# Six weight matrices turned by VectorE from 32x32 blocks instead of by TensorE, in a transformer block on one Trainium2 core

## The chip, the cores and the metric

The kernel runs on one core of one Trainium2 chip. The metric is device time in microseconds (us) for one execution. The core has five engines that each work through their own instruction list in order: TensorE (PE; its weight loads are listed as PEld), VectorE (DVE), ScalarE (ACT), GpSimd (POOL) and SyncE (SP). They wait for each other by semaphores. DMAs are issued here from SP's list, some at the start from ACT's.

## What is computed

The input x is 16 sequences of 256 tokens with 256 features, all in float32. Each sequence goes through attention with 16 heads, a conditioned RMS norm, an RWKV-like mixing with a scan along the tokens, a rotation, and a gated feed-forward net of 704 hidden units whose inputs and weights are first rounded to blockwise FP4 (16 neighbours share a scale):

```
q, k, v = x @ Wq.T, x @ Wk.T, x @ Wv.T              # 256x256 each
a  = softmax(mask(q k^T / 4)) v @ Wo.T              # 16 heads of 16
xn = rmsnorm(a) * scale * (1 + sc) + shift          # shift, sc from silu(cond) @ Wc.T + bc
x1 = x + wkv(xn; Wk, Wv, Wr, decay, first) @ Wo2.T  # the second set of 256x256 weights
h  = silu(fp4(xr) @ fp4(w_gate).T) * (fp4(xr) @ fp4(w_up).T)   # xr = x1 filtered and rotated; 704x256 weights
out = x1 + fp4(h) @ fp4(w_down).T                   # 256x704
```

Every weight is used transposed, with its input feature on the partitions, so each has to be turned once on the way in.

## The kernel before

The 16 sequences ("batches" b) are pipelined through stages, all written as generators that yield after a few instructions: `ask` (a: load the next x, project q, k, v), `attend` (t), `leave` (l: output projection and norm), `mix` (m), `rotate` (r), `hidden` (h and i, two row halves), `turn_h` (d and e) and `down` (f). Set-up stages bring in the constants: `loads` (L: issue the DMAs of weights and small vectors), `turn_w` (Q for q, k, v; O for o; A for the second set), `turn_mask` (K), `modulate` (M), `rotation` (R), `times` (T), `in_weights` (W0 to W5: gate and up, quantised and turned) and `out_weights` (V0, V1: down).

The string ORDER, written out at the top of the file by a planner, names the stage that is to take its next step. A loop under a manual schedule walks through it, so each engine's list is ORDER's projection on that engine. Nothing reorders it at run time. The instruction that waits holds up everything behind it on its engine.

The lines that the change and the prediction touch (numbers of the kernel before):

- **L143, `load_x`.** x of a batch comes in as four DMAs of 32 partitions with rows of 64 floats (256 bytes). In that layout each 32x32 block lies where VectorE's 32x32 transpose (L605) turns the whole of it into feature-major xT in one instruction. The x buffer has two slots.
- **L216, `load_w`.** The weights q, k, v, o come in as one DMA of 256 KB each with rows of 1 KB, in SP's list. **L224 to L227**: 13 small DMAs of vectors and of the conditioning (tile `rows`) in ACT's list.
- **L301 and L305, `turn_w`.** Four TensorE transposes of 128x128 turn a weight into PSUM and one copy brings it to SBUF: on VectorE for q, k, v, o (L305), on ScalarE for the second set ak, av, ar, ao (L307).
- **L524 to L535, `in_weights`.** Gate and up (1408 rows in all) are taken 256 rows at a time, six times: 12 DMAs, `quant` on 512 columns (the last on 256), 22 TensorE transposes (L531), six ScalarE copies into guT (L535).
- **`quant`, L488 to L500.** First half on VectorE: absolute maximum, scale, reciprocal, multiply (L488, L490, L491, L492). Then ScalarE takes the absolute value into bf16 (L494). Second half on VectorE: two roundings (L496, L497). POOL multiplies the scale back (L500).
- **L313, L315**: `rows` turned by TensorE and copied to `cols`, from which most of the set-up starts. **L318, L323, L329**: the mask made float, turned, reduced. **L352 to L358**: silu of the conditioning on VectorE, and the matmuls that need it. **L433, L439**: the rotation matrix.
- **L567, L579, L656, L677**: projections, scores and attention values on TensorE. The first L579 on oT is `leave(0)`.

The weight tiles borrow buffers that later hold other things. `raw` (gate, up, down on their way in) shares its two buffers with the mask in float.

The build hands the DMAs eight completion semaphores in turn. A DMA's issue waits until the DMA eight places before it (in the program's order over both lists) has landed, so at most eight are in flight.

At the start TensorE runs 12 transposes of the identity matrix into a bank that nobody reads (L184).

Of the kernel before, what the change touches and what calls it, by code (L numbers as in the profile page):

```python
# [27 lines left out]
L L L L W1 L Q Q L K L a0 W5 a0 W1 W1 K K Q Q Q W1 Q a0 L W1 a0 R a0 K a0 L W5 R L W0 W1 K K K W5 A R t0 a0 L A  # L28
W1 O t0 L a0 W3 R W5 W5 W0 M a1 A O t0 A W5 a1 R M a2 W5 t0 t0 t0 a1 R a1 t0 W0 W3 t0 R W3 W3 t0 W2 a1 t0 t0 a1
M a1 t1 a1 W0 A W3 V0 t1 t1 R R A M t0 W0 W3 a2 R t1 W0 V0 M t1 W2 t1 t0 W3 t1 t1 W4 a3 V1 W0 t0 A t0 M t0 t1 V0  # L30
t0 a3 t0 A T W2 W2 t1 T t1 V0 t1 a2 a2 a2 t1 l0 a2 t1 a2 t1 V0 l0 l0 t1 V0 a2 W4 W2 t1 l0 V0 a4 l0 l0 t2 l0 m0
t1 V1 W4 a3 t2 t2 a3 a3 m0 m0 m0 m0 m0 t2 t2 a3 W4 V1 t2 m0 m0 m0 l1 l1 l1 m0 m0 m0 l1 t2 W4 m0 m0 m0 m0 m0 t2
t2 t2 t2 l1 V0 l1 l1 a3 a3 V0 t2 t2 r0 V1 t2 W4 m1 m1 t2 W2 m1 m1 r0 a4 m1 t3 m1 W4 t3 t2 m1 m1 V1 t2 t3 t3 t2
W2 V1 r0 t3 t3 m1 m1 m1 m1 r0 V1 a4 l2 l2 m1 m1 m1 m1 t3 m1 a4 r0 t3 l2 t3 t3 a4 t3 t3 l2 r1 r1 r0 t3 r0 a4 l2
t3 t3 r1 r1 r1 l2 l2 a4 a4 a5 t3 r0 r0 a5 r0 m2 m2 t4 t4 t3 t3 m2 m2 a6 i0 i0 i0 i0 t4 i0 i0 i0 i0 i0 i0 i0 i0
i0 i0 m2 m2 m2 m2 m2 r1 r1 r1 r1 m2 t4 t4 m2 t4 r1 m2 a5 a5 a5 a5 a5 a5 m2 l3 t5 l3 t4 l3 l3 h0 m2 m2 m2 t4 t5
m2 h0 h0 h0 h0 h0 h0 l3 h0 h0 h0 r2 t5 l3 l3 V1 h0 i1 h0 r2 t4 r2 a6 V1 h0 m3 t4 i1 a7 h0 r2 i1 h1 i1 r2 t4 h1
h1 i1 t4 h1 t4 t4 h1 h1 h1 t4 m3 m3 a6 h1 h1 t5 a6 h1 r2 h1 r2 t4 t5 t4 i1 a6 r2 r2 t5 h1 h1 i1 r2 m3 a6 t5 i1
i1 i1 i1 t5 t5 h1 m3 t5 t4 t5 t5 a6 a6 m3 m3 t6 t6 m3 m3 m3 i1 i1 m3 m3 i2 i2 i2 i2 i2 m3 e0 e0 i2 i2 t6 t6 e0
i2 l4 i2 t6 i1 i2 i2 t6 h2 h2 e0 t5 m3 m3 m3 l4 h2 t6 l4 h2 m3 h2 t6 l4 h2 i2 h2 h2 h2 h2 t5 r3 h2 t5 l4 r3 a7  # L40
d0 l4 t5 h2 t6 t5 t5 l4 i2 m4 d0 d0 m4 a8 h2 t6 d0 h2 i2 a7 r3 t6 a7 a7 t6 t6 t6 t6 a7 m4 m4 m4 r3 r3 a7 a7 m4
m4 m4 t7 l5 t7 t7 l5 m4 m4 m4 m4 m4 t6 t7 l5 l5 l5 r3 m4 m4 e1 m4 m4 l5 l5 t7 t6 t6 f0 f0 f0 f0 r4 t7 r3 r4 a8
r3 e1 e1 e1 r3 f0 t7 t7 t7 d1 d1 r4 t7 t7 d1 r3 r4 i3 a9 d1 r4 i3 m5 m5 i3 i3 i3 i3 i3 a8 r4 m5 m5 i3 i3 i3 t7
a8 a8 a8 i3 i3 i3 m5 m5 t8 m5 m5 m5 l6 l6 a8 a8 l6 r4 h3 h3 l6 t8 t8 m5 h3 h3 h3 f1 m5 m5 t8 t8 i3 l6 t8 h3 f1
m5 m5 h3 h3 t7 r4 r4 r4 f1 l6 m5 m5 l6 h3 h3 h3 m5 t8 t8 t7 t7 t7 t7 t8 r5 t8 f1 t8 i4 i4 m6 t8 t8 r5 a9 d2 h3
h3 i4 d2 i4 aa i4 t8 m6 h3 t8 m6 a9 r5 r5 r5 a9 a9 a9 t8 t9 t7 d2 r5 r5 t8 t9 m6 i4 d2 r5 r5 r5 i4 i4 i4 i4 e2
m6 e2 m6 a9 i4 e2 i4 t8 e2 a9 m6 m6 l7 i4 l7 m6 m6 m6 t9 l7 l7 f2 f2 m6 m6 m6 m6 l7 l7 l7 l8 l8 t9 h4 m7 h4 l8
h4 m6 l8 m6 m7 f2 h4 f2 h4 h4 h4 h4 r6 h4 h4 l8 m7 m7 t9 t9 r6 l8 l8 h4 t9 t9 t9 r6 aa e3 f1 r6 i4 i5 h4 t9 e3
e3 e3 h4 i5 i5 i5 i5 t9 m8 r6 i5 m7 i5 i5 h4 r6 aa m7 i5 aa t9 t9 t9 ab t9 m8 i5 i5 i5 d3 f2 m7 r6 d3 h5 h5 h5
h5 h5 aa aa h5 i5 r6 r6 ta t9 h5 t9 h5 m7 h5 ta ta h5 h5 m7 h5 aa ta r6 h5 m8 aa m7 d3 d3 m7 m7 m7 m7 h5 m7 f3  # L50
m7 m7 f3 f3 f3 m8 m8 ta ta ta m8 ta m8 ta r7 r7 m8 m8 m8 ta ta d4 d4 ta i5 ta ta ta ab f3 i6 i6 i6 i6 i6 i6 i6
i6 i6 i6 i6 h6 h6 h6 h6 h6 h6 h6 h6 h6 h6 i6 ab ab ab ab d4 d4 ta tb h6 m8 h6 t9 m8 e4 e4 i6 h6 ab m8 ta ta e4
m8 ac r7 m8 l9 tb m8 i6 ab e4 f4 f4 l9 r7 h6 r7 f4 l9 l9 l9 m8 e5 tb r8 tb f4 l9 l9 f4 r8 d5 ac m9 m9 m9 r8 e5
r8 r7 r7 tb m9 la d5 r7 la la m9 m9 r8 la ac ac m9 m9 m9 m9 m9 r8 r7 tb m9 d5 m9 r7 ac m9 la d5 la la m9 ac tb
m9 tb tb i7 ma ma tb tb ad i7 i7 i7 i7 i7 i7 i7 i7 e5 e5 i7 i7 i7 tb tc tc tc m9 r8 i7 f5 f5 i7 ma f5 f5 d6 f5
r8 d6 r9 tb h7 r9 tb h7 ad r8 tb ma r8 h7 h7 h7 h7 r9 r9 h7 h7 h7 ma ma tb r9 ma r9 tc tc tc tb h7 h7 h7 ad ad
tb r9 ac ac ma ma ma ma ma h8 h8 h8 tc ma ma d6 h8 h8 d6 tc ad i8 ma ma ad r9 i8 i8 i8 i8 i8 i8 h8 h7 h8 tc i8
i8 i8 h7 ma h8 e6 h8 e6 e6 e6 h8 lb h8 h8 r9 f6 lb i8 i8 r9 f6 h8 f6 f6 ra i8 lb lb lb f6 tc tc ra e7 lb lb e7
tc h8 i8 i9 tc i9 i9 i9 ae tc ra tc mb e7 i9 mb ad ra ra td d7 e7 i9 ad tc ra i9 ae d7 td td mb mb ra tc i9 tc
i9 mb td td h9 ra i9 mb i9 mb td mb h9 mb h9 i9 h9 h9 h9 mb h9 h9 h9 d7 d7 td h9 h9 td td i9 h9 h9 lc lc td lc  # L60
af mb ae ra mb lc f7 mb mb i9 ae lc lc ra mb f7 mb lc mc ia mc h9 ia ia ia ia f7 f7 ia ia ia td ia ia ia ia mb
rb rb td td d8 td ae rb f7 ia td rb ae ae mc d8 te td mc d8 mc ae rb ia d8 rb td e8 mc td mc mc af mc e8 e8 e8
mc mc mc rb mc ld mc mc f8 te mc te te rb rb ld ld ld te ha f8 f8 ha mc ha ha rb te ha f8 ha ha ha te ha ib ha
ha ha te te te te te ib ha rc ib ib ib ib ib ib ld ld ld te rc ha ib rc ib ib e9 hb d9 rc md e9 af te rc md hb
ib hb f8 te hb md hb ib e9 md d9 af te te af e9 hb rc rc ib rc te C md af hb hb hb hb hb d9 d9 tf md af af md rc
rc hb hb le le md md tf f9 tf le md md f9 le md tf md md md md md tf tf ic ic ic ic ic f9 f9 ic ic ic le hb rd
ic le ic tf ic rd le ic me f9 rd tf ic da tf rd rd da ea hc ea hc hc rd ea ic me hc da ea tf hc rd hc tf da me
me me me tf tf hc rd me hc hc tf tf hc hc me me hc me tf tf rd tf hc me fa me me me me fa fa rd db fa me lf id
db lf fa id id id id lf lf id id id me db id id id hc lf C hd hd lf db hd lf id hd hd eb re id eb eb hd hd mf mf
id eb hd re re hd fb re hd dc hd re fb fb mf re dc fb hd mf fb mf mf re hd mf ec ec ec dc dc mf ec re fc hd mf  # L70
fc mf fc mf mf ed re fc dd fc ed mf re dd mf mf mf mf ed ie ed ie ie ie ie ie ie ie dd rf dd ie ie he C he ie he
rf rf ie C rf he ie he ie he rf fd he he he rf rf rf fd he fd he rf ee fd rf if if he he if ee if if he if if if
if hf hf if hf if if hf ee ee fd hf if hf de if hf hf hf de de de hf hf fe hf hf fe hf fe fe ef ef ef fe ef df
df df df ff ff ff ff ff
# [4 lines left out]
def kernel(  # L79
# [58 lines left out]

    def load_x(b):
        if b < B:  # L140
            t = io.tile([P, S // 32, 64], F32, tag="x", name="x_sb", bufs=2)
            for a in range(4):
                queue[0].dma_start(  # L143
                    out=t[32 * a : 32 * a + 32], in_=x[b].rearrange("(q i) (a c) -> a i q c", i=32, a=4)[a]
                )
            x_sb[b] = t
# [36 lines left out]
    for i in range(12):  # L183
        nc.tensor.transpose(warm[:, 0:P], ident, ident)  # L184
# [24 lines left out]
    def loads():  # L209
        def load_w(name, src, tag, bufs=1):  # L210
            w_in[name] = lent(tag, bufs)
            if name == "ao":

                nc.sync.dma_start(out=w_in[name], in_=src.rearrange("(p h) c -> p h c", h=2))
            else:
                nc.sync.dma_start(out=w_in[name], in_=src.rearrange("(t p) c -> p t c", p=P))  # L216
# [3 lines left out]
        load_w("q", w_q, "ek")  # L220
        yield
# [10 lines left out]
        yield  # L232
        load_w("v", w_v, "kv")
# [58 lines left out]
    def turn_w(*names):  # L292
        for name in names:
            t = w_in.pop(name)
            pt = ps()
            for ct in range(E2):
                for ot in range(E2):
                    part = t[:, ot, ct * P : (ct + 1) * P]
                    if name in ("q", "k", "v"):
                        part = half(t[:, ot, :], ct)  # L300
                    nc.tensor.transpose(pt[:, ct * E + ot * P : ct * E + (ot + 1) * P], part, ident)  # L301
            yield
            wT[name] = wts.tile([P, E2, E], F32, tag="wt_" + name, name="wt_" + name)
            if name in ("q", "k", "v", "o"):
                nc.vector.tensor_copy(flat(wT[name]), pt)  # L305
            else:
                nc.scalar.copy(flat(wT[name]), pt)  # L307
            yield
# [205 lines left out]
    def in_weights(j):  # L514
        j *= 2 * P
        nt = min(2, (2 * FF - j) // P)
        n = nt * E
        raw = wk.tile([P, FF], F32, tag="h", name="raw", bufs=2)[:, 0:n]
        for jj in range(nt):
            lo, hi = j + jj * P, j + (jj + 1) * P  # L520
# [434 lines left out]
    for j in range(6):  # L955
        stages[f"W{j}"] = lambda j=j: in_weights(j)
# [159 lines left out]
```

## Time and profile before

| what | value |
|---|---|
| time, median of 3 runs | 677.73 us (676.33 to 678.62) |
| the profiled execution: its own time | 678.29 us |
| the profiled execution: its span | 676.4 us (1.9 us of the time lie around it) |
| granted TensorE clock, mean | 0.998 |
| DMA moved | 13.63 MB in 37,327 packets, 32,900 of them under 512 bytes |
| busiest TensorE lines | L880 (gate and up) 163.9 us, L656 (scores) 74.0, L934 (down) 70.7, L677 (values) 61.7 |
| transposes that the change concerns, on TensorE | L301 on q, k, v, o: 16; L531 on gate and up: 22 |
| last TensorE instruction ends | at 671.1 us |

How to read it: a busy time is the sum of an engine's instructions. The chain of waits follows the last instruction back, at each step to what released it, and so shows which engine set the end. A window table gives each engine's busy time in a stretch. TensorE's instructions overlap, so a mean duration of one (0.27 us for a 128x128 transpose late in the set-up) is longer than its share of the chain (0.11 us).

### The profile page before, as it was taken

The page shows a single profiled execution, that of the slowest core. Times are in us where ns is not written, and L with a number is a line of the kernel's source. Part 1 is how long each engine was busy: PE and PEld are TensorE (multiplying, and loading weights), DVE is VectorE, ACT ScalarE, POOL GpSimd, SP SyncE. Part 2 cuts the span into 40 slices and gives each one's busy share as a digit, 9 for nine tenths or more (in the row PEclk, how much of TensorE's full clock was granted, in tenths as well). Part 3 has the DMA queues.
Part 4 walks back from the last instruction along what each step waited for, and adds up shares of the span by engine and source line. Part 5 has one row for each costly group of instructions (what it writes and reads, how often), then busy time and mean ns, then how long its engine had stood idle before and what let it go on. Part 6 is the DMA issues. An engine that isn't in the chain of part 4 may idle for free.

```text
span 676.4 us, 10441 instructions
## 1 busy us (share of the span) xinstructions
PE 662.4 (98%) x3928; PEld 467.7 (69%) x3928; DVE 580.9 (86%) x973; ACT 353.7 (52%) x777; POOL 147.0 (22%) x171
## 2 busy tenths in 40 slices
PE   6999999999999999999999999999999999999995
PEld 5667666756677766866777767676776677768774
DVE  6887988998897868888989898898998898999971
ACT  1788756564574465555344644273454554343232
POOL 4802311311222021130203120130311313031210
PEclk9999999999999999999999999999999999999999
DMA  5520000000001001010010100010000000001001
GB/s 160 131 69 1 9 9 17 1 16 0 1 17 29 5 1 32 1 25 9 5 28 1 32 5 12 1 32 1 16 1 17 1 0 17 1 16 31 10 9 36
DMA packets 37327, 13.63 MB, mean 20 GB/s; under 512 B 32900, under 2 KB 36884, under 8 KB 37268
## 3 DMA queue, kind: packets, MB, share of 16 engines
q1 hardware_dynamic: 37152, 12.85, 7.6%
q8 instruction: 33, 0.54, 0.3%
q14 instruction: 26, 0.21, 0.1%
q10 hardware_dynamic: 116, 0.02, 0.0%
HBM read 8.67 MB, written 4.19 MB: 19 GB/s over the span
## 4 chain that ended last, share of the span: by engine, by line
PE 90%; DVE 6%; DMA 1%; ACT 1%; issue 0%; SPq 0%; POOL 0%; ACTq 0%; POOLq 0%; DVEq 0%
PE ps L567 24%; PE ps L880 21%; PE pss L656 10%; PE ps L934 9%; PE ps L677 9%; PE ps L579 8%; PE ps L543 3%; PE ps L843 2%; PE ps L917 2%; PE ps L591 1%; DVE v L496 1%; DVE v L497 1%; DVE h L897 1%; DVE am L488 1%; PE ps L301 1%; DVE v L492 1%
## 5 line engine op out<-in xcount | busy, mean ns | idle before, releaser
L880 PE MATMUL ps<-guT,xqT 128*128 128x352 f32 x512 | 163.9, 463 | 0.5 <-ACT xqT L865 0.3
L665 ACT ACTIVATE w<-pss 128x512 f32<-128x512 f32 x256 | 133.7, 606 | 41.5 <-PE pss L656 41.3
L880 PEld LDWEIGHTS ps<-guT,xqT 128*128 128x128 f32 x512 | 94.1, 190 | 55.0 <-issue 3.7
L500 POOL TENSOR_TENSOR hq<-v,am 128x704 f32<-128x704 f32 (+2 forms) x40 | 56.0, 1401 | 203.0 <-DVE v L497 147.0
L656 PE MATMUL pss<-qT,kT 32*128 32x512 f32 x512 | 74.0, 640 | 0.0
L934 PE MATMUL ps<-hT,downT 128*128 128x256 f32 x312 | 70.7, 380 | 0.0
L494 ACT ACTIVATE m<-v 128x704 bf16<-128x704 f32 (+2 forms) x56 | 40.7, 729 | 50.1 <-DVE v L492 40.8
L934 PEld LDWEIGHTS ps<-hT,downT 128*128 128x128 f32 x312 | 58.9, 190 | 10.1 <-DVE h L897 0.8
L677 PE MATMUL ps<-w,v_one 128*32 128x256 f32 x1024 | 61.7, 382 | 0.0
L891 ACT ACTIVATE th<-ps 128x352 f32<-128x352 f32 x64 | 30.2, 472 | 56.2 <-PE ps L880 54.3
L814 DVE RECIPROCAL den<-den 128x512 f32<-128x512 f32 x16 | 53.6, 3348 | 0.5
L496 DVE SCALAR_TENSOR_TENSOR v<-m,v 128x704 f32<-128x704 bf16 (+2 forms) x56 | 47.1, 841 | 5.1 <-ACT m L494 5.1
L677 PEld LDWEIGHTS ps<-w,v_one 128*32 128x32 f32 x1024 | 30.1, 109 | 29.4 <-issue 6.3
L497 DVE SCALAR_TENSOR_TENSOR v<-m,v 128x704 f32<-128x704 bf16 (+2 forms) x56 | 47.1, 841 | 1.9
L546 ACT COPY hT<-ps 128x384 f32<-128x384 f32 (+1 forms) x64 | 27.1, 431 | 40.1 <-PE ps L543 40.0
L893 DVE SCALAR_TENSOR_TENSOR th<-th,ps 128x352 f32<-128x352 f32 x64 | 32.4, 506 | 13.3 <-ACT th L891 13.0
L897 DVE SCALAR_TENSOR_TENSOR h<-th,ps 128x352 f32<-128x352 f32 x64 | 33.3, 520 | 8.2 <-PE ps L880 3.9
L500 POOL TENSOR_TENSOR xq<-v,am 128x512 f32<-128x512 f32 x16 | 18.5, 1154 | 87.4 <-DVE v L497 87.4
L543 PEld LDWEIGHTS ps<-ident,hq 128*128 128x128 f32 (+1 forms) x204 | 23.5, 136 | 18.7 <-issue 4.9
L656 PEld LDWEIGHTS pss<-qT,kT 32*128 32x128 f32 x512 | 20.7, 182 | 22.6 <-issue 18.6
L817 POOL TENSOR_TENSOR yT<-num,den 128x512 f32<-128x512 f32 x16 | 20.6, 1288 | 71.1 <-DVE den L814 56.3
L687 DVE STREAM_TRANSPOSE u<-ps 128x512 f32<-128x512 f32 x32 | 22.5, 704 | 14.3 <-PE ps L677 14.3
(175 smaller groups left out, 1191.9 us busy)
## 6 DMA issues: line engine op xcount, KB each, us to landing
x_sb<-in_x_dram SPq DMA_DIRECT2D x64, 64.0 KB, 2.1
out_dram<-o_sb SPq DMA_DIRECT2D x52, 64.0 KB, 1.8
out_dram<-o_sb SPq DMA_DIRECT2D x6, 128.0 KB, 3.9
raw<-in_L_ffn_w_down_dram SPq DMA_DIRECT2D x2, 352.0 KB
raw<-in_L_ffn_w_gate_dram SPq DMA_DIRECT2D x5, 128.0 KB, 3.0
raw<-in_L_ffn_w_up_dram SPq DMA_DIRECT2D x5, 128.0 KB
ek<-in_L_cond_Wq_dram SPq DMA_DIRECT2D x1, 256.0 KB, 3.0
er<-in_L_cond_Wk_dram SPq DMA_DIRECT2D x1, 256.0 KB
```

The source lines that it names most:

```text
L496: nc.vector.scalar_tensor_tensor(v, m, 1.5 * 2.0**22, v, ALU.max, ALU.add)
L497: nc.vector.scalar_tensor_tensor(v, m, 1.5 * 2.0**22, v, ALU.max, ALU.subtract)
L500: nc.gpsimd.tensor_tensor(blk(dst), blk(v), bc(am), ALU.mult)
L543: nc.tensor.transpose(pt[0:n, (k - k0) * P : (k - k0 + 1) * P], src[:, k * P : k * P + n], ident)
L567: nc.tensor.matmul(pool_tile[:, ot * n : (ot + 1) * n], w[:, ct, ot * P : (ot + 1) * P], src[ct], start=(ct == 0), stop=(ct == E2 - 1),)
L579: nc.tensor.matmul(pool_tile[:, tt * E : (tt + 1) * E], srcT[:, ct, tt * P : (tt + 1) * P], w[:, ct, :], start=(ct == 0), stop=(ct == E2 - 1),
L656: nc.tensor.matmul(quad[r], kT[rows_, g, kt * P : (kt + 1) * P], qT[rows_, g].rearrange("p i q -> p (i q)"), start=True, stop=True,)
L665: nc.scalar.activation(w[:, kt, r].rearrange("p i q -> p (i q)"), quad[r], AF.Exp)
L677: nc.tensor.matmul(pu[32 * r : 32 * r + 32, i * S : (i + 1) * S], vo[:, kt, 8 * g + 2 * r + i, :], w[:, kt, r, i, :], start=(kt == 0), sto ...
L814: nc.vector.reciprocal(flat(den), flat(den))
L880: nc.tensor.matmul(p_[:, 0:FH], xqT[:, ct, tt * P : (tt + 1) * P], guT[:, ct, base + f * FH : base + (f + 1) * FH], start=(ct == 0), stop= ...
L934: nc.tensor.matmul(pdn[:, 0:S], downT[:, k, h * P : (h + 1) * P], hT[:, k, :], start=(k == 0), stop=(k == FK - 1))
```

## The change

Weights q, k, v are loaded like x, in four DMAs of 32 partitions with rows of 256 bytes, and turned by one VectorE transpose each. q and v are issued from ACT's list, v right behind q and ahead of the 13 small vectors; k stays on SP. Weight o is loaded in eight DMAs with rows of 128 bytes and also turned by one VectorE transpose. Gate and up are taken in four parts of 352 rows instead of six of 256: four DMAs each with rows of 256 bytes, `quant` on 704 columns, one VectorE transpose straight into guT, no TensorE and no PSUM. The second set (ak, av, ar, ao) and down are as before. The 12 idle transposes become 18. ORDER is another one throughout.

```diff
+    def in_blocks(t, src, engine):
...
+        for a in range(4):
+            engine.dma_start(out=t[32 * a : 32 * a + 32], in_=src.rearrange("(q i) (a c) -> a i q c", i=32, a=4)[a])
...
-    for i in range(12):
+    for i in range(18):
         nc.tensor.transpose(warm[:, 0:P], ident, ident)
...
+            elif name in ("q", "k", "v"):
+                in_blocks(w_in[name].rearrange("p t (q c) -> p (t q) c", c=64), src, nc.sync if name == "k" else nc.scalar)
+            elif name == "o":
+                for a in range(4):
+                    for h in range(2):
+                        nc.sync.dma_start(
+                            out=w_in[name].rearrange("p t (q h j) -> p h (t q) j", h=2, j=32)[32 * a : 32 * a + 32, h],
+                            in_=src.rearrange("(q i) (h a j) -> a h i q j", i=32, h=2, a=4)[a, h],
+                        )
...
+            if name in ("q", "k", "v"):
...
+                nc.vector.transpose(
+                    as_blocks(flat(wT[name])), by_blocks(t.rearrange("p t (q c) -> p (t q) c", c=64))
+                )
...
+            if name == "o":
...
+                nc.vector.transpose(
+                    as_blocks(flat(wT[name])), t.rearrange("p t (q h j) -> p h (t q) j", h=2, j=32)
+                )
...
-            if name in ("q", "k", "v", "o"):
-                nc.vector.tensor_copy(flat(wT[name]), pt)
-            else:
-                nc.scalar.copy(flat(wT[name]), pt)
+            nc.scalar.copy(flat(wT[name]), pt)
...
     def in_weights(j):
...
+        src = (w_gate, w_up)[j // 2][(j % 2) * FH : (j % 2 + 1) * FH]
+        raw = wk.tile([P, FF], F32, tag="h", name="raw", bufs=2)
+        in_blocks(raw.rearrange("p (q c) -> p q c", c=64), src, nc.sync)
+        yield
+        wq = yield from quant(raw, FF, "hq", 4)
+        nc.vector.transpose(
+            guT[:, :, j * FH : (j + 1) * FH].rearrange("p h (q i) -> p h q i", i=32),
+            by_blocks(wq.rearrange("p (q c) -> p q c", c=64)),
+        )
...
-    for j in range(6):
+    for j in range(4):
         stages[f"W{j}"] = lambda j=j: in_weights(j)
```

The new order changes the lists at the start as follows. In SP's list stand x of batch 0, k, one quarter of gate and up (W1), the mask, x of batch 1, the eight DMAs of o, Wc, ak, av, then W0, x of batch 2, W3, ar, ao. In VectorE's list the first half of W1's `quant` stands ahead of the copy of `cols` and of the mask. In TensorE's list the first projections follow the idle transposes directly, and the silu matmuls stand ahead of the transposes of ar, where they stood behind the rotation's matmuls.

## The prediction

> **What bounds the kernel now.** I read the page first, for which engine is full and where.
>
> ```profile
> span 676.4 us, 10441 instructions
> ...
> PE 662.4 (98%) x3928; PEld 467.7 (69%) x3928; DVE 580.9 (86%) x973; ACT 353.7 (52%) x777; POOL 147.0 (22%) x171
> ...
> PE   6999999999999999999999999999999999999995
> ```
>
> TensorE is busy in every slice but the first and the last. Windows of 15 us (stretch, its length, then busy us of PE, PEld, DVE) sharpen this for the set-up:
>
> ```profile
> 15.00:30.00 15.00, 15.00 (x111) 10.25 (x110) 12.14 (x35) 11.84 (x24) 11.98 (x34) 1.00 0.51 133
> 30.00:45.00 15.00, 15.00 (x138) 9.70 (x141) 12.37 (x28) 12.36 (x27) 3.89 (x3) 1.00 0.31 81
> 45.00:60.00 15.00, 15.00 (x105) 10.04 (x98) 13.16 (x24) 11.57 (x26) 4.28 (x5) 1.00 0.09 22
> ```
>
> PE has 15.00 of 15, and so on to 585 us with 0.1 us missing; after that it loses 1.5 us up to 660 and ends with the last batch's serial tail. So from 15 us on, an instruction taken from TensorE is time saved, and each new wait of TensorE is time lost. VectorE is the next engine, at 12 to 13 of 15. TensorE's waits at the start are the other reserve:
>
> ```profile
> PE ps L301 <- DMA ek<-in_L_cond_Wq_dram: 1.7, 1, 1.7
> PE ps L301 <- DMA kv<-in_L_cond_Wv_dram: 1.5, 1, 1.5
> ```
>
> Last the chain of waits (start, length, what), which is TensorE's list after 11 us. I use three of its marks:
>
> ```profile
> 12.14 4.93 PE ps L567 x16
> ...
> 34.08 0.59 PE ps L301 x4
> ...
> 50.52 3.65 PE ps L579 x16
> ```
>
> 12.14 is the first projection. 34.08 is the point by which TensorE has done the work that the new order puts before the silu matmuls. 50.52 is `leave(0)`. Up to there the new order has the same work, in another sequence, without the transposes: 8 sets of scores, 3 of values, projections of three batches, the second set of weights. I compare the kernels at this mark.
>
> **What goes.** On TensorE, 38 transposes. Twelve (q, k, v) lie in the waiting start. In the chain four of o cost 0.44 us, and the 14 L531 before the mark 0.47 + 0.24 + 0.47 + 0.67 = 1.85 us. The 8 L531 behind it, at 0.117 each (0.47 / 4), are 0.94. So 3.2 us leave the full part of TensorE. ScalarE loses six L535 (3.3 us) and is not the bound.
>
> **What comes to VectorE.** Four copies L305 at 0.68 become four transposes at 0.70 (L605, same shape): 0. Four transposes into guT, 704/512 x 0.694 (L867, strided the same way) = 0.95 each: +3.8. `quant` of gate and up on 704 columns costs 0.854 + 0.202 + 0.428 + 0.893 = 2.4 for a first half and 0.90 + 0.945 = 1.85 for a second (rows of the form 704): 4 x 4.25 = 17.0, against 19.3 for the six parts before. Net +1.5 us, in the stage where VectorE has least room. No row shows a transpose of 704 columns: not below the 512's 0.70, and not above 0.9 + 0.25 (a 704-column pass plus the spread of the rows), so all four lie between 2.8 and 4.6. The six more idle transposes run from 5.2 to 6.6 us (0.235 apart as in the row of L184), before anything else is ready: nothing.
>
> **When the set-up can start.** Each DMA issue takes 0.45 us and 0.05 to the next. The first x DMA landed 2.4 us after its issue ended (1.13 to 3.51); the x rows of the first 60 us say
>
> ```profile
> DMA to landing us min/median/max: 2.2/2.6/3.6
> ```
>
> I take 2.4 from issue to landing, with 2.2 and 3.6 as ends. Small vectors took 1.2 (mix_r, issued at 3.53, released the next DMA at 4.76) to 2.8 (cond). With eight semaphores, issues are chained by landings. x is issued from 0.72 to 2.6 with q beside it; the last lands at 4.7; the last DMA of k is issued there and lands at 7.1; a small vector behind it lands at 8.4; the last DMA of W1 is then issued at 9.0 and lands at **11.5**. Nothing hides this: before, VectorE began W1 at 9.36. TensorE can project q at about 7.1 (VectorE's L265 holds it to 5.6, then two transposes), 5 us sooner than 12.14, but this is not passed on. ScalarE's list has 8 + 13 issues ahead of qT; the last vector waits for W1's third DMA (10.9), so qT starts at 11.2, kT is ready at 13.1, and the first scores at 13.1 stand against 18.42. Loading o in eight DMAs of 128-byte rows is hidden (o is needed at `leave(0)`), except for its seven more issues in SP's list, counted below; POOL's list only exchanges six L500 (7.1 us) for four (5.7).
>
> **VectorE's list, which I expect to set the pace.** Its new wait is W1's first half (L488 on `raw`) for the landing at 11.5; queued behind are `cols` and the mask, for which TensorE waits, then all of the set-up. Durations are from the timeline and the groups by form. From 11.5: W1's first half 2.4, cols 0.19, mask 0.43, L386 to L391 1.4, second half 1.85, keep 0.69, xT 0.70, v_one 0.6, some and mgain 1.3: 9.6, to 21.1. SP meanwhile issues x of batch 1 until 11.8, then o, Wc, ak, av (11 issues, to 17.8), W0 to 19.8, x to 21.8, W3 to 23.8. W0 lands at 21.8 and W3 at 25.8, each making VectorE wait (and ScalarE's L494 behind W3, with the exponentials queued after it): W0's first half ends at 24.2, W3's at 28.2. Then guT 0.95, L347 0.64, u 0.72, xT 0.70, second half 1.85, silu 1.5 (32.98 to 34.49 before): 6.4, to **34.6**.
>
> TensorE, by chain lengths, would be at the silu matmuls at 30.9: scores from 13.1, mask 14.5 to 15.0, v and scores to 18.0, ak landed at 19.8 (issued at 16.8, 3.0 for 256 KB), to 20.2, two projections 3.84, av and Wc 0.88, values 1.86, scores 1.07, v 1.92, scores 1.07. So it waits 3.7 us for VectorE. This is the new wait. Before, that pair had slack:
>
> ```profile
> 32.98 1.02 DVE L352 TENSOR_SCALAR sil<-sil 64x16 f32<-64x16 f32 x1
> ...
> 37.94 1.06 PE L358 MATMUL ps<-sil,x1T 64*128 64x16 f32 x8
> ```
>
> From 34.6 to `leave(0)` VectorE has division 1.2, shift and gain 1.2, L433 1.3, W3's second half 1.85, two first halves 4.8, two guT 1.9, rotP 0.4, two u 1.4, wt_o 0.7, division 1.2 and gaps 0.3: 16.0. TensorE's share of the same stretch is 14.7 (silu 1.0, ar and ao 0.9, three scores 3.2, rotation 0.95, two values 3.7, q and k 3.8, scores 1.1). So VectorE sets it: `leave(0)` at 34.6 + 16.0 = **50.6**, against 50.52. Behind it TensorE is ahead again: VectorE's next 9.4 us up to the first mix stand against 11.5 on TensorE.
>
> **Sum.** 50.6 - 50.52 - 0.94 = -0.9 us: 678.3 becomes 677.4 in the profiled execution's own terms. The median of the runs lies 0.6 below that execution, so 676.8, rounded to **677**. The tail has the same list in both orders and counts for nothing.
>
> **A rule against part of it.** x rows of 256 bytes moved 137 GB/s at a DMA share of 0.58 (25.0 to 25.5 us), 236 at full share; the weights with rows of 1 KB moved 274 at 0.86, 319. The Trainium skill, "DMA: Bandwidth & Descriptors", Specifications, asks 512 bytes and more for line rate, and its section "Issuing engines are not separate DMA queues" holds that issuing from several engines saves only issue time. The first agrees with these rows and would cost 1.4 MB about 1.5 us of DMA time if rate were the limit. By the second, q and v on ACT gain 8 issues of 0.5 at most.
>
> **Rivals.**
> *TensorE stays the bound* (26%). If W1 lands by 9.5 and W0 and W3 ahead of VectorE, VectorE never holds TensorE, and `leave(0)` comes at 30.9 + 14.7 = 45.6: -5.9 us, 671.8 by the median. Partial relief gives 672 to 675. For it: VectorE had 1 to 2 us gaps before 60 us. Against it: W1's chain of three landings and a vector.
> *Landings at the upper row* (25%, slower). With 3.6 instead of 2.4 (x's maximum, and the row of ak), three landings put W1 at 15 and VectorE's chain, with its two waits partly absorbing it, 3 us later: +2.1, 680. It decides once W1 lands after about 14; below that the result is within 0.3%. TensorE's pauses could add to it: after the pauses of the start, the first eight L567 took 3.41 us (from 11.94) where eight took 1.89 from 15.19 on. One such slow stretch behind a pause, where TensorE and not VectorE is late, costs 1.5: 682. (The Trainium skill, "TensorE: Matmul & The Clock Gate", Part 1, lets the clock fall after an idle window of about 3.4 us; the pause of 3.7 at the silu matmuls is of that length.)
> *No net effect by design* (4%): the planner's order elsewhere gives or takes what the set-up brings.
> *VectorE sets the mark* as worked out: 45%.
>
> **How the numbers follow.** 0.3% is about 2 us, what a measurement of this kernel can tell from no change. The forecast's own spread, 674.5 to 679.5 (landing 2.2 to 2.9), is mostly within that; of its 45% and the 4%, 9 lie below 675.7 and 4 above 679.8. Faster: 26 + 9 = 35%. Slower: 25 + 4 = 29%. Same: 36%. The range reaches from the first rival's end to the second's with the clock: 671.8 to 682.
>
> **What will show it.** Right: first scores on TensorE at 13 to 14 us; TensorE's waits headed by the silu matmuls waiting for VectorE, 2 to 5 us; VectorE's L509 on raw waiting for DMAs; `leave(0)` near 50 to 51; TensorE full after 55. Wrong: no wait of TensorE above 1 us after 21 us (first rival), W1's first half starting after 14 us (second), or losses behind 60 us, which nothing here predicts.

## The result, and the profile after

The changed kernel takes **681.93 us** (median of 20 runs, 678.11 to 684.26 but for one of 1733.75 that nothing here explains) against 677.89 (20 runs, 676.33 to 679.23): ratio **1.0054**, 95% interval 1.0038 to 1.0070. It is slower. The forecast was 677.0; its range just holds the result, its sign was wrong.

The runs are not one heap. Four of the 19 lie between 678.1 and 678.4 at a mean granted clock of 0.995 to 0.996, the others between 680.4 and 684.3 at 0.994 down to 0.985. The profiled execution is one of the slowest, 683.84 us with a span of 682.0. The page of it:

```profile
span 682.0 us, 10394 instructions
...
PE   6889999999999999999999999999999999999995
...
PEclk8979999999999999999999999999999999999998
```

Two things stand in it: TensorE is below 9 in two more slices than before, and the granted clock is below 9 in the first slice, the third and the last, where it was 9 throughout before. The windows of 15 us (stretch, length, busy us of PE, PEld, DVE, ACT, POOL, clock, DMA share, GB/s) say where:

```profile
15.00:30.00 15.00, 13.09 (x96) 9.11 (x93) 10.00 (x26) 8.91 (x17) 12.68 (x34) 0.93 0.82 174
30.00:45.00 15.00, 12.61 (x54) 7.88 (x52) 13.68 (x27) 8.78 (x20) 2.77 (x2) 0.66 0.31 71
45.00:60.00 15.00, 15.00 (x147) 10.04 (x147) 13.70 (x24) 11.34 (x25) 2.84 (x3) 1.00 0.09 25
```

Before, PE had 15.00 in each. Now 1.9 are idle in the first and 2.4 in the second, and the second has a mean clock of 0.66, so what was busy there took longer too. TensorE's waits (line waited for, us, times, longest):

```profile
PE ps L323 <- DMA den<-in_L_attn_Wk_dram: 1.9, 1, 1.9
PE ps L379 <- DVE sil L375: 1.8, 1, 1.8
PE ps L334 <- DMA rows<-_cond_spectral_gate_dram: 1.6, 1, 1.6
```

The first is ak coming in from memory, the second the silu matmuls waiting for VectorE, as forecast, the third the small vectors ahead of the first scores. The chain behind that wait (start, length):

```profile
36.35 1.86 PE ps L379 x8
38.21 1.04 PE ps L323 x4
39.25 2.02 PE pss L666 x8
...
54.66 3.65 PE ps L589 x16
```

The eight silu matmuls took 0.99 us before, four transposes of a weight 0.59, eight scores 1.07. Each takes nearly double here. `leave(0)`, the mark of the prediction, comes at 54.66 where it was 50.52. Finer windows show the clock's fall as a block:

```profile
34.00:36.00 2.00, 0.52 (x1) 0.00 (x0) 1.93 (x4) 1.90 (x4) 1.21 (x1) 0.51 0.57 130
36.00:38.00 2.00, 1.65 (x8) 1.68 (x8) 1.24 (x4) 0.00 (x0) 0.18 (x1) 0.50 0.02 4
...
44.00:46.00 2.00, 2.00 (x25) 0.94 (x28) 1.90 (x5) 0.76 (x3) 0.00 (x0) 0.93 0.25 30
```

It is 1.00 up to 34, 0.50 to 44 and 1.00 again: some 10 us at half rate, the last 8 of them with TensorE full. The fall begins before the wait for VectorE does (windows of 0.5 us, then TensorE's list):

```profile
33.50:34.00 0.50, 0.50 (x3) 0.01 (x1) 0.47 (x2) 0.50 (x3) 0.00 (x0) 1.00 0.28 106
34.00:34.50 0.50, 0.50 (x1) 0.00 (x0) 0.50 (x1) 0.50 (x2) 0.00 (x0) 0.55 0.54 122
```

```profile
31.76 2.76 PE L666 MATMUL pss<-qT,kT 32*128 32x512 f32 x8 [0.56 <-ACT w L675]
36.35 1.86 PE L379 MATMUL ps<-sil,x1T 64*128 64x16 f32 x8 [1.83 <-DVE sil L375]
```

A mean of 0.55 over 0.5 us puts the fall at 34.05. The eight scores that began at 31.76, behind a pause of 0.56 us, ran until 34.52 (2.76 us, with waits in between, where the others of this stretch take 1.14), and the wait of 1.8 us at the silu matmuls starts only there. VectorE's list, last, where W0 and W3 begin (in brackets the idle time ahead and what ended it):

```profile
24.30 0.89 DVE L509 TENSOR_REDUCE am<-raw 128x44 f32<-128x704 f32 x1 [3.65 <-DMA raw<-in_L_ffn_w_gate_dram]
27.85 0.89 DVE L509 TENSOR_REDUCE am<-raw 128x44 f32<-128x704 f32 x1 [0.90 <-DMA raw<-in_L_ffn_w_up_dram]
```

### The profile page after: what moved, and what is told of

It is laid out like the page before. It is cut to its first block, busy times and chain, and to the rows that moved or that the text cites. A ratio compares the mean times of both kernels' runs of the same rounds, so it can differ in the third digit from the quotient of the medians.

```text
span 682.0 us, 10394 instructions
## 1 busy us (share of the span) xinstructions
PE 663.6 (97%) x3896; PEld 467.4 (69%) x3896; DVE 580.4 (85%) x965; ACT 351.5 (52%) x769; POOL 142.8 (21%) x169
## 4 chain that ended last, share of the span: by engine, by line
PE 90%; DVE 4%; SPq 2%; DMA 2%; ACT 1%; issue 1%; ACTq 0%; POOL 0%; POOLq 0%; DVEq 0%
PE ps L577 24%; PE ps L890 21%; PE ps L944 10%; PE pss L666 10%; PE ps L687 8%; PE ps L589 8%; PE ps L553 3%; PE ps L853 2%; PE ps L927 2%; SPq L141 1%; PE ps L601 1%; SPq L222 1%; DMA ek<-in_L_cond_Wq_dram 0%; DVE den L824 0%; DMA kv<-in_L_cond_Wv_dram 0%
## 5 line engine op out<-in xcount | busy, mean ns | idle before, releaser
L521 POOL TENSOR_TENSOR hq<-v,am 128x704 f32<-128x704 f32 x38 | 54.6, 1438 | 212.7 <-DVE v L518 165.6
L666 PE MATMUL pss<-qT,kT 32*128 32x512 f32 x512 | 76.5, 655 | 0.8 <-ACT w L675 0.6
L515 ACT ACTIVATE m<-v 128x704 bf16<-128x704 f32 (+1 forms) x54 | 40.1, 746 | 44.3 <-DVE v L513 44.3
L518 DVE SCALAR_TENSOR_TENSOR v<-m,v 128x704 f32<-128x704 bf16 (+1 forms) x54 | 50.2, 929 | 1.9
L517 DVE SCALAR_TENSOR_TENSOR v<-m,v 128x704 f32<-128x704 bf16 (+1 forms) x54 | 44.6, 826 | 3.6 <-ACT m L515 3.6
L521 POOL TENSOR_TENSOR xq<-v,am 128x512 f32<-128x512 f32 x16 | 18.1, 1133 | 89.6 <-DVE v L518 89.6
L827 POOL TENSOR_TENSOR yT<-num,den 128x512 f32<-128x512 f32 x16 | 22.0, 1374 | 66.0 <-DVE den L824 55.0
L553 PE MATMUL ps<-ident,hq 128*128 128x128 f32 (+1 forms) x204 | 32.2, 276 | 1.9 <-POOL hq L521 1.5
```

Source lines behind the costliest of these rows:

```text
L517: nc.vector.scalar_tensor_tensor(v, m, 1.5 * 2.0**22, v, ALU.max, ALU.add)
L518: nc.vector.scalar_tensor_tensor(v, m, 1.5 * 2.0**22, v, ALU.max, ALU.subtract)
L521: nc.gpsimd.tensor_tensor(blk(dst), blk(v), bc(am), ALU.mult)
L553: nc.tensor.transpose(pt[0:n, (k - k0) * P : (k - k0 + 1) * P], src[:, k * P : k * P + n], ident)
L666: nc.tensor.matmul(quad[r], kT[rows_, g, kt * P : (kt + 1) * P], qT[rows_, g].rearrange("p i q -> p (i q)"), start=True, stop=True,)
```

## Theories and experiments

**Theory A:** two costs. W0 and W3 land late, because o's eight DMAs stand ahead of them, and in the pauses that this leaves TensorE, its clock falls. **Theory B:** VectorE's added work sets the set-up, whatever lands when. **Theory C:** the loss is in the new order behind the set-up. They are compared in one table. "Ratio" is to the kernel before, measured beside it (its medians there: 677.9 to 678.8). A row of an experiment rests on 6 to 12 runs, but e4 and e6 on 4 and e11 on 5. The last columns are of the profiled execution: its own time, the start of the silu matmuls and of `leave(0)` in TensorE's list (0.07 us before the chain's), and the time less the latter.

| kernel | median us | ratio (95%) | own time | silu | `leave(0)` | rest |
|---|---|---|---|---|---|---|
| before | 677.73 | | 678.29 | 37.94 | 50.45 | 627.8 |
| after | 681.93 | 1.0054 (1.0038 to 1.0070) | 683.84 | 36.35 | 54.59 | 629.3 |
| e1_fill | 680.17 | 1.0028 (1.0017 to 1.0040) | 680.37 | 37.47 | 52.76 | 627.6 |
| e2_olast | 677.37 | 0.9988 (0.9970 to 1.0007) | 676.19 | 32.03 | 49.61 | 626.6 |
| e3_tailfill | 680.78 | 1.0037 (1.0022 to 1.0052) | 678.26 | 35.92 | 51.18 | 627.1 |
| e4_old_qkvo | 684.78 | 1.0094 (1.0080 to 1.0109) | 685.33 | 44.90 | 57.41 | 627.9 |
| e5_old_gu | 679.50 | 1.0016 (1.0007 to 1.0025) | 679.40 | 38.41 | 51.12 | 628.3 |
| e6_old_both | 687.90 | 1.0141 (1.0121 to 1.0160) | 687.89 | 45.81 | 60.21 | 627.7 |
| e8_olast_mid | **675.57** | **0.9960 (0.9945 to 0.9975)** | 675.11 | 33.21 | 48.50 | 626.6 |
| e9_olast_mid_tail | 675.49 | 0.9961 (0.9946 to 0.9976) | 674.40 | 32.17 | 47.46 | 626.9 |
| e10_long_rows | 680.65 | 1.0041 (1.0026 to 1.0056) | 679.80 | 35.64 | 53.13 | 626.7 |
| e11_qv_sp | 684.95 | 1.0100 (1.0083 to 1.0117) | 681.77 | 37.73 | 53.92 | 627.9 |
| e12_o_plain | 679.91 | 1.0021 (1.0009 to 1.0032) | 680.79 | 35.72 | 54.16 | 626.6 |
| e13_warm12 | 676.16 | 0.9974 (0.9960 to 0.9988) | 675.56 | 32.08 | 47.37 | 628.2 |
| e14_fill_silu | 678.91 | 1.0017 (1.0004 to 1.0030) | 680.63 | 37.72 | 53.05 | 627.6 |
| e15_fill_v | 680.88 | 1.0035 (1.0019 to 1.0052) | 677.62 | 35.59 | 50.85 | 626.8 |

**Theory C falls by the last column.** The mark moves over 12.8 us between these kernels, the rest stays within 626.6 to 628.3, in the changed kernel's profile alone 629.3. Nearly all that moves the time happens before `leave(0)`.

### Work in TensorE's pauses: e1_fill, e14_fill_silu, e15_fill_v

```diff
# e1: 22 and 10; e14: the first alone, 14; e15: the second alone, 10
         pm = ps()
+        for _ in range(22):
+            nc.tensor.transpose(pm[:, 4 * NB : 4 * NB + P], ident, ident)
         for t in range(4):
...
         pv = ps()
+        if b == 1:
+            for _ in range(10):
+                nc.tensor.transpose(pv[:, 0:P], ident, ident)
         project_rows(pv, wT["v"], xT)
```

Expected of e1: 

> The changed kernel with idle transposes in TensorE's list where it waits: 10 ahead of the v projection of batch 1 and 22 ahead of the silu matmuls, into PSUM columns that the real matmuls overwrite or leave alone. Theory 1 (TensorE's clock falls while it waits, and the slow stretch behind the wait is the larger loss): the granted clock stays at 1.00 from 30 to 45 us, the wait for VectorE stays about as long, leave(0) starts at 52 instead of 54.6, and the median falls by 2 to 3 us, to about 679.3. Theory 2 (VectorE's lateness alone is the loss): leave(0) stays at 54 to 55 and the time at 682 or a little above, since 3.5 us of work are added.

Expected of e14: 

> The changed kernel with 14 idle transposes (1.6 us) ahead of the silu matmuls alone, shorter than the 1.8 us for which TensorE waited there. Theory (of the 4.9 us between forecast and median, some 3.7 are the clock, which falls in most executions in the pauses of 31 to 36 us; those executions of the changed kernel that end at 678.1 to 678.4 are the ones without it): filling the last pause keeps the clock, the silu matmuls' eight take about 1 us, and the runs lie at 678 to 679.5, without the upper group at 681.7 to 684.3. Rival (the clock has already been let fall by the waits inside the scores before): both groups remain, median 681 to 682.5.

Expected of e15: 

> The changed kernel with 10 idle transposes (1.2 us) ahead of batch 1's v projection alone, in front of the scores that wait for the exponentials; the pause of 1.8 us at the silu matmuls stays. If the pause at the silu matmuls decides whether the clock falls: two groups remain and the median is 681 to 682.5. If it is the work done in the several us before, however spread: fewer upper runs and a median of 679 to 680.5.

e1's profile has the clock at 1.00 throughout 30 to 45 us and the silu matmuls at 0.99 us again; all ten runs lie within 679.38 to 681.34. But 22 transposes are more than the pause held: no wait is left at the silu matmuls, which begin 1.1 us later than without them (0.6 of it because VectorE was ready at 36.84 instead of 36.20). So e14 fills only 1.6 us. Nine of its 12 runs lie at 678.2 to 679.7, two at 680.0 and 680.6 and one at 683.0. Its profile shows that the clock still falls, though more briefly:

```profile
34.00:36.00 2.00, 2.00 (x10) 1.46 (x8) 1.93 (x4) 2.00 (x5) 0.97 (x1) 0.61 0.55 125
36.00:38.00 2.00, 2.00 (x11) 1.67 (x10) 1.48 (x4) 0.14 (x1) 0.42 (x1) 0.54 0.05 10
38.00:40.00 2.00, 2.00 (x20) 1.46 (x19) 1.06 (x7) 0.55 (x1) 0.00 (x0) 1.00 0.00 0
```

Summed over both rows that is 3.4 us at half rate, of which the idle transposes took most, where the changed kernel had 10 us, all but some 2 of it in real work. This fall begins at 34.42, before the idle transposes do (34.6), so they did not prevent it: the stretch at half rate was shorter and fell on useless work. Theory A holds in what the clock costs: 1.6 us of useless work in one pause brings the median down from 1.0054 to 1.0017 of before, 2.5 us. In e15 both groups remain, four runs at 677.6 to 678.2 and eight at 680.6 to 683.3 (the median, 680.88, just misses the 681 given for this case). Work in the pause before the scores does not remove the upper group, work ahead of the silu matmuls nearly does. Even so the pause only makes a fall likely: e3 below is the same kernel as after up to the tail, and its profile caught an execution without that fall, the silu matmuls at full rate behind a pause longer than after's:

```profile
35.92 1.03 PE L379 MATMUL ps<-sil,x1T 64*128 64x16 f32 x8 [1.90 <-DVE sil L375]
```

It ended at 678.26, like the four lowest times of after. A fall of its clock lay at 22 to 25 us, where TensorE had slack before the wait for VectorE. Theory B falls with these and with e2 below, where the loads land sooner: VectorE's work is the same in all of them.

### o's load behind ao's, or as one DMA: e2_olast, e12_o_plain

```diff
# e2: load_w("o", ...) moved behind load_w("ao", ...)
-        load_w("o", w_o, "num")
-        yield
...
         load_w("ao", a_o, "yT", 2)
         yield
+        load_w("o", w_o, "num")
+        yield
# e12: o in its place, by one DMA, turned by TensorE and a VectorE copy
-            elif name == "o":
-                for a in range(4):
-                    for h in range(2):
...
```

Expected of e2: 

> The changed kernel with the load of o moved behind all other loads of its stage (behind ao). Nothing else moves. Theory 1 (o's eight issues of 0.5 us in SP's list delay ak, W0 and W3, these delay VectorE, and its lateness opens the pause in which the clock falls): ak lands 3 us sooner and TensorE's wait for it (1.9) goes; VectorE starts W0 at 21 instead of 24.3 and W3 at 24.5 instead of 27.9; silu ready at 33 instead of 36.2; leave(0) at 48 to 50; time 675 to 677, below the kernel before. Theory 2 (VectorE's extra work sets the pace, not the DMAs): silu ready no sooner than 35, time 680 to 682.

Expected of e12: 

> The changed kernel with o loaded, in the same place of SP's list, by one DMA with rows of 1 KB and turned by four TensorE transposes and a VectorE copy, as before the change. Theory (o's seven more issues and its short rows stand ahead of ak, W0 and W3 and make them late): ak, W0 and W3 come 2 to 3.5 us sooner, as with o's DMAs moved behind, and the median is 677 to 679. Rival (o's place matters but not its form: 256 KB ahead of ak delay it as much in either form): W0 and W3 within 0.7 us of 24.3 and 27.9 and a median of 681 to 682.5.

With o behind, VectorE finds W0 and W3 3.1 and 3.4 us sooner:

```profile
21.17 0.89 DVE L509 TENSOR_REDUCE am<-raw 128x44 f32<-128x704 f32 x1 [0.23 <-DMA raw<-in_L_ffn_w_gate_dram]
24.43 0.89 DVE L509 TENSOR_REDUCE am<-raw 128x44 f32<-128x704 f32 x1 [0.60 <-DMA raw<-in_L_ffn_w_up_dram]
```

The silu matmuls start at 32.03 instead of 36.35 (3.4 us of it from W3, 1.0 from L375, see the end) and the time is 677.37, by the ratios 4.5 us less, though the clock still fell (0.77 in 30 to 45). o in its old form gains less than I expected, W0 1.9 and W3 0.9 us sooner and 679.91: SP's list reaches W0 3.4 us sooner (15.52 for 18.91), but there the four DMAs of x of batch 2 take 3.38 us of it instead of 1.95, which I read as waiting for a place among the eight in flight. So o's seven extra issues are about half of its price (2.2 of 4.5 us by the ratios); the other half is its place.

### Rows and queues of the loads: e10_long_rows, e11_qv_sp

```diff
# e10
-        in_blocks(raw.rearrange("p (q c) -> p q c", c=64), src, nc.sync)
+        rows = src.rearrange("r c -> (r c)").rearrange("(p n) -> p n", n=FF)
+        for a in range(4):
+            nc.sync.dma_start(out=raw[32 * a : 32 * a + 32], in_=rows[32 * a : 32 * a + 32])
# e11
-                in_blocks(w_in[name].rearrange("p t (q c) -> p (t q) c", c=64), src, nc.sync if name == "k" else nc.scalar)
+                in_blocks(w_in[name].rearrange("p t (q c) -> p (t q) c", c=64), src, nc.sync)
```

Expected of e10: 

> The changed kernel with gate and up read in the same four DMAs of 32 partitions and 88 KB, but each partition from one unbroken row of 2816 bytes instead of 11 rows of 256 (the weights come out in another arrangement, so what is computed differs; every instruction stays). Theory (the rate of short rows makes W0 and W3 land late): the first halves of W0 and W3 start 1 to 2.5 us earlier than 24.3 and 27.9, the silu matmuls with them, and the median is 679.5 to 681. Rival (number of DMAs in flight and their order, not row length): W0 and W3 within 0.5 us of where they were, median 681.5 to 682.5.

Expected of e11: 

> The changed kernel with q and v issued from SP's list like k, in the same places of the order; ScalarE issues none of the weights. Theory (ScalarE's list saves eight issues of 0.5 us in SP's): SP is up to 4 us later with everything behind, the first half of W1 starts 1 to 4 us after 12.0 and the median is 683 to 685. Rival (the issues are chained by landings anyway, so the second list gains nothing): W1 within 0.5 us of 12.0 and a median within 1 us of 682.

Long rows bring W0 to 22.79 and W3 to 26.98, 1.5 and 0.9 us sooner:

```profile
22.79 0.89 DVE L509 TENSOR_REDUCE am<-raw 128x44 f32<-128x704 f32 x1 [2.74 <-DMA raw<-in_L_ffn_w_gate_dram]
26.98 0.89 DVE L509 TENSOR_REDUCE am<-raw 128x44 f32<-128x704 f32 x1 [1.69 <-DMA raw<-in_L_ffn_w_up_dram]
```

So rate did count there: in the changed kernel the DMA engines' share is 1.01 from 18.5 to 21 us, 1.31 to 23 and 1.04 to 25, at 254, 218 and 174 GB/s, with nothing in hand. At the silu matmuls 0.7 us of it are left, and the intervals of the ratios overlap, so a gain in time is not shown. With q and v on SP too, W1 starts at 14.35 instead of 12.02 and 3 us are lost, as the theory of ScalarE's list said. That list is the part of the change that pays without doubt.

### The blocks in the old order: e4_old_qkvo, e5_old_gu, e6_old_both

The kernel before with its own ORDER, all loads on SP, and q, k, v, o (e4), gate and up in six parts (e5), or both (e6) by blocks and VectorE:

```diff
# e4 and e6
+            elif name in ("q", "k", "v"):
+                in_blocks(w_in[name].rearrange("p t (q c) -> p (t q) c", c=64), src, nc.sync)
+            elif name == "o":
+                for a in range(4):
+                    for h in range(2):
...
# e5 and e6, for each part of 256 rows
+        nc.vector.transpose(
+            guT[:, :, j : j + nt * P].rearrange("p h (q i) -> p h q i", i=32),
+            by_blocks(wq.rearrange("p (q c) -> p q c", c=64)),
+        )
```

Expected of e6: 

> The kernel before, with its own order and its 12 idle transposes, but q, k, v, o and gate and up loaded as 32x32 blocks (all from SP's list) and turned by VectorE; gate and up stay in six parts of 256 rows. It is the change without the new order and without ScalarE's queue. If the method as such is sound: TensorE is 3.2 us lighter behind 12 us, 674 to 675. If the many DMAs, eight in flight and half a microsecond each to issue, are the trouble: SP's list grows by some 28 issues (14 us) in the first 25 us, the last parts of gate and up land 10 us later, VectorE waits for them with other work behind, and the time is 680 or more.

Expected of e4: 

> The kernel before, its order kept, with q, k, v, o alone loaded as blocks (20 DMAs on SP for four) and turned by VectorE. Theory (in the old order the price of the blocks is their issues, 0.49 us each in SP's list ahead of ak, of which the list with both kinds of blocks had 36 in a row): 16 more issues, 7.9 us later by SP's list, against the 3.1 us by which TensorE waited there before; 3 to 6 us slower than before: 681 to 684. Rival (the short rows or VectorE's work are the price, so gate and up, three times the bytes, carry most): within 1 us of before, 677 to 679.5.

Expected of e5: 

> The kernel before, its order kept, with gate and up alone loaded as blocks (28 DMAs for 13, all six parts as before) and turned by VectorE. Theory of the issues: the first parts W1 and W5 bring 3 to 6 more issues ahead of ak, 1.5 to 3 us; the time is 678 to 681, and with the other half they add up to the 9.6 us that both together cost. Rival (short rows or VectorE's work): 5 to 9 us slower, 683 to 687.

Together they cost 9.6 us, q, k, v and o alone 6.6 (more than I expected), gate and up alone 1.3, in sum 7.9 and not the 9.6 expected. The transposes taken from TensorE are there paid for in SP's list. From e6's (start, length, DMAs):

```profile
12.98 3.90 SPq L224 DMA_DIRECT2D num<-in_L_cond_Wo_dram  x8
16.93 1.93 SPq L147 DMA_DIRECT2D x_sb<-in_x_dram  x4
...
21.30 0.51 SPq L229 DMA_DIRECT2D den<-in_L_attn_Wk_dram  x1
```

ak (den) is issued at 21.30, where it was 11.93 before, and TensorE waits 5.0 us for it. Each issue takes 0.49 us with its gap and they stand shoulder to shoulder: the issues, not the landings, set the pace. The new order, four parts of gate and up for six, and ScalarE's list win back 5.6 to 6.0 of the 9.6 (by each kernel's own before, or by the two medians).

### Tail, start, and the best version: e3_tailfill, e13_warm12, e8_olast_mid, e9_olast_mid_tail

```diff
# e8: e2's move, with 10 idle transposes ahead of the silu matmuls and 8 ahead of batch 1's v projection
# e13: e8 with for i in range(12) for the first idle transposes; e9 and e3: e8 and after with 12 more in the last batch's
     def turn_half(src, dst, k0, fill=0):
         pt = ps()
+        for _ in range(fill):
+            nc.tensor.transpose(pt[:, 0:P], ident, ident)
```

Expected of e3: 

> The changed kernel with 12 idle transposes in the tail, ahead of the last batch's last transposes, where TensorE waits 1.5 us for POOL. If the fall of the clock in the profiled tail (0.50 from 669 to 672) is part of the loss: it goes, and the median falls by 0.5 to 1.6 us. If it is a chance of the profiled execution, which the kernel before has as often: no more than 0.5 us.

Expected of e8: 

> The changed kernel with o's eight DMAs behind those of ao, and with 8 idle transposes ahead of batch 1's v projection and 10 ahead of the silu matmuls. Theory (two separate costs: late landings behind o's DMAs, and a TensorE clock that falls in the pause they leave): both go. With o moved alone the silu matmuls began at 32.0 and leave(0) at 49.7 with TensorE at 0.77 of its clock from 30 to 45 us; with the clock kept I expect leave(0) at 46.5 to 47.5 and a median of 674 to 676, narrow. Rival (VectorE sets the mark in any case, so the clock is only slack): leave(0) at 49 to 50 and a median of 677 to 678 as with o moved alone.

Expected of e9: 

> The kernel with o behind and the idle transposes in the set-up, and 12 idle transposes more in the first half of the last batch's turned hidden rows. If the clock also falls in the last batch's serial tail in most executions (1.65 us in the changed kernel's profile), 1 to 1.5 us less than the same kernel without them: 673 to 674.5. If it falls there only now and then, or if the idle transposes delay what follows: no difference, or 0.5 to 1 us more.

Expected of e13: 

> The kernel with o behind and the idle transposes in the set-up, its 18 idle transposes at the very start cut back to the 12 of the kernel before. If the six only fill a wait, no difference: within 0.7 us of the same kernel with 18 (675.6 beside a before of 678.8, ratio 0.996). If they keep the clock up for the first projections: q's projection at half rate, 1 to 2 us later there, of which the landing of W1 hides all but 0.5; ratio 0.996 to 0.998.

e8 is faster than both kernels, by 0.40% than before. Its windows:

```profile
15.00:30.00 15.00, 15.00 (x108) 10.65 (x104) 13.36 (x32) 11.47 (x23) 13.36 (x33) 0.93 0.85 169
30.00:45.00 15.00, 14.32 (x137) 8.64 (x137) 14.46 (x29) 10.88 (x24) 4.43 (x4) 1.00 0.38 95
45.00:60.00 15.00, 15.00 (x102) 10.73 (x101) 13.83 (x25) 12.39 (x29) 3.13 (x4) 1.00 0.08 19
```

TensorE is full again but for 0.7 us, and at full clock from 30 us on. `leave(0)` was expected at 46.5 to 47.5 and came at 48.5; e9's profile, which differs only in the last batch, has 47.46: there L375 took 0.17 us, in e8's 1.29 beside a POOL product, and that is the microsecond. Fill in the tail makes no difference that stands out of the noise: the intervals of e9 and e8 overlap, and those of e3 and after. The 12 or 18 idle transposes at the start can't be told apart either.

## Why the prediction was wrong

**Right.** The first scores, forecast at 13.1, came at 13.32, W1's first half at 12.0 for 11.5; q's projection ran at 7.36 for 7.1. VectorE transposes of 704 columns took 0.87 to 0.91 us (0.95 forecast). The silu matmuls became a wait for VectorE, of 1.8 us (3.7 forecast). Behind the mark, 627.8 was to become 626.9 by the eight L531; the median of the table's last column over the eleven variants of the changed kernel is 626.9.

**"W0 lands at 21.8 and W3 at 25.8": the landing term of 2.4 us.** VectorE found them at 24.30 and 27.85. The profile gives these DMAs 3.1 to 3.2 us from issue to landing (3.9 for W0's four), ek and kv 3.0 to 3.1, against the 2.4 that I took from x alone, whose rows stood in a less crowded stretch. I had set the short rows' rate aside ("if rate were the limit"); at a share of 1.0 to 1.3 it was, as e10 shows. The Trainium skill, "DMA: Bandwidth & Descriptors", Specifications, asks 512 bytes and more for line rate: the 0.9 to 1.5 us that e10's long rows gain agree with it. What I cited of the same page on issuing engines, that a second list saves issue time only, was worth 3.0 us (e11), of at most 4 that I gave it. VectorE was 1.6 us later at the silu matmuls (36.2 for 34.6). Alone this leaves the result at the four lowest times, 678.1 to 678.4, some 1.2 above the forecast and within 0.3% of before (e3's profile, without the fall of the clock there, ended at 678.26).

**"TensorE's share of the same stretch is 14.7 ... So VectorE sets it".** This is the step that failed: TensorE sets the mark. VectorE's transpose that makes oT, and the start of `leave(0)`, first in after, then in e3, whose clock was full there:

```profile
51.44 0.45 DVE L712 STREAM_TRANSPOSE oT<-on 128x256 f32<-128x256 f32 x1
54.59 1.99 PE L589 MATMUL ps<-wt_o,oT 128*128 128x256 f32 x8
```

```profile
49.97 0.45 DVE L714 STREAM_TRANSPOSE oT<-on 128x256 f32<-128x256 f32 x1
51.18 1.99 PE L591 MATMUL ps<-wt_o,oT 128*128 128x256 f32 x8
```

In profiles with a full clock (e1, e3, e8, e13, e15) TensorE takes 15.3 us from the silu matmuls to `leave(0)`, not 14.7, and still comes 0.8 us after oT is ready. VectorE's stretch, forecast at 16.0 (its terms as written add up to 16.25), took 14.65 in e3, and 15.7 in after, where 0.94 of it is a wait for the slow silu matmuls. In after TensorE took 18.2, for 10 us of it ran at half clock: VectorE had oT ready at 51.9, TensorE came to it at 54.6. The fall cost 2.9 us at the mark (18.2 for 15.3), and another in the last batch added 1.65 (TensorE's matmuls at 0.62 of the clock from 668 to 672). The forecast had a term for it, in the second rival: "One such slow stretch behind a pause, where TensorE and not VectorE is late, costs 1.5: 682." Its price came from the start of before, where the profile lists a clock of 1.00, and so from no recorded fall. The mechanism was named, and mis-sized twice: it was an add-on to another case, where 15 of 19 runs lie above the four lowest, at a lower mean clock; and it was one stretch, where the profile has three on end (see below). That the result lies beside this 682 is luck in part, for the rival's own condition, W1 after about 14 us, was not met (12.0). Over the runs the fall is worth up to 681.9 less 678.2, 3.7 us, of which e14's fill alone gives back 2.5.

**"The tail has the same list in both orders and counts for nothing."** A share of the 2.4 us that the profiled execution lost behind the mark is the clock again (1.65). The rest, a pause for POOL's hq of 1.46 us for 1.16 among it, was not followed up, as no experiment moved it.

What stays open: why the fall strikes one execution and not the next of the same kernel. The Trainium skill, "TensorE: Matmul & The Clock Gate", Part 1, has a free-running window of about 3.4 us, which would make it a matter of phase. The lengths and beginnings below agree with that, and the phase differs from profile to profile; no run sets it.

## What to carry to other kernels

A saving of instructions on the bound engine is worth what its replacement's DMAs leave of it: count issues (0.49 us each here) and landings ahead of every load that the critical engine waits for, and put loads that are needed late (o, needed at 50 us) last in the list. Short pauses of TensorE can cost more than their length, as the clock may halve around them (here for 3.4 to 10.2 us); a few idle transposes, fewer than the pause holds, are a cheap test of that, and the shape of the runs (two groups) shows it before any trace does. Sum the stage once with each engine as the bound: where two sums are within 10%, as 16.0 and 14.7 were here, their errors decide.

## What the runs showed of the hardware

- **The clock fell behind a pause of 0.6 us and waits inside the scores, not behind one long idle time:** in after at 34.05 us, with no gap of TensorE over 0.56 us in the 3.4 us before. The page named above has the clock fall after an idle window of about 3.4 us; this fall differs from that.
- **Falls come in multiples of one length.** From the mean clock of 30 to 46 us, at half rate: 3.5 us in e14 and e11, 6.7 in e2 and e10, 10.2 in after and e12. Within one profile they also begin on one grid: in after at 13.57, 34.05, 668.93 and 679.17 us, which are 6, 186 and 3 times one length of 3.413 us apart (665.6 us for 195 of them); in e11 at 9.10, 22.75, 39.82 and 667.87, which are 4, 5 and 184 times that. The unit agrees with the skill's 3.4 us. The skill has the clock back after at least one busy window; after stayed low for 8 us of full work.
- **Small VectorE passes beside POOL work can be slow:** the 64x16 product L375 took 1.17 us in after, beside POOL's 128x704 product L521 (34.79 to 36.18), and 0.17 in e2, where L521 came after it. In all nine profiles in which it took 1.17 to 1.29 us it ended within 0.04 us of POOL's product; in e9 and e13, as in e2, that product came later and it took 0.17. It stands on the path to the silu matmuls.
- **While o's eight DMAs with rows of 128 bytes were being issued, 73 GB/s were moved at a DMA share of 0.47** (15.0 to 17.2 us of after); between 20 and 21 us, with ak and av (rows of 1 KB) and the first of W0's DMAs in flight, it was 320 at 1.00.
